# Cross attention on one core: the hand-written order of the first batch rewritten, one step of the last batch moved, nine warming products instead of ten

## The chip, the cores and the metric

The kernel runs on one core of one Trainium2 chip. The metric is the device time of one execution in microseconds (us). The engines of the core work side by side, each through its own list in order: TensorE (PE, matrix products into PSUM banks), VectorE (DVE), ScalarE (ACT), GpSimd (POOL, here reductions across partitions and accumulating transfers) and SyncE (SP, which issues most transfers). They wait for one another through semaphores.

## The reference

Eight batches of one cross-attention layer, all in float32. `x` and the context are (8, 512, 1024).

```python
q = jnp.einsum('bcn,dc->bnd', x1, Wq) + bq
k = jnp.einsum('bcn,dc->bdn', x2, Wk) + bk[:, None]
v = jnp.einsum('bcn,dc->bdn', x2, Wv) + bv[:, None]
attn = jax.nn.softmax(jnp.einsum('bnd,bdm->bnm', q, k), axis=2)
attn_out = jnp.einsum('bcm,bnm->bcn', v, attn)
return attn_out + x1
```

The width of q and k is 64, the softmax runs over the 1024 positions m, in eight blocks of 128.

## The kernel before, in words

A batch is a set of small steps, each a method of class `Batch` of one or a few instructions. Three strings, FIRST (batch 0), MIDDLE (batches 1 to 6) and LAST (batch 7), list the steps in program order; `follow` (called at the end of the kernel function) runs through the words. A word is a step and its indices; "+" ahead of it means the next batch, "-" the one before. The scheduling is manual: what the strings say is each engine's order. Two words on different engines have no order between them but that of their data and buffers.

The steps, by engine:

- TensorE. `VF.j.c` (line 373) is a float32 product for value block j in the first batch, one quarter c of the contraction, two recorded products each; blocks 0, 1 and 2 of batch 0 go this way. All other values take three passes of float32r with operands split in parts: `VY.j` (one pass, four products into a Y bank) and `VX.j` (two passes, eight products into an X bank). `K` and `Q` (line 204) project keys and queries with 64 output columns. `S.h.i` (line 261) makes scores of query half h and key block i. `RF.u.m` (line 458) is the float32 product of weights and values for query units 0 and 1 of batch 0; `R.u.m` (line 433) does three passes for the others.
- ScalarE. `wh`, `w4`, `xh`, `H`, `vh`, `qr`, `kr` round the high parts. `ke` and `qe` take K and Q out of PSUM. `Sc` copies scores to SBUF (line 266). `E` is the exponential (line 292), `es.Q` copies half of a query quarter Q for its sum, `sy` seeds a Y bank with the bias (line 389), `cy` and `oy` take Y banks out, `r2`, `of`, `os` scale.
- VectorE. `wl`, `wd`, `xl`, `xd`, `vl`, `vd`, `l`, `d`, `ql`, `kl` make the low and the combined parts. `jf` and `jn` join the banks to a value block. `F.Q` folds the scores of a quarter to a maximum (lines 274 to 277), `L.u` subtracts the maximum from unit u (line 289), `a2` and `a3` add up (line 318), `rec` inverts (line 337), `o` joins an output (line 498).
- POOL. `T.Q` reduces the maximum over the partitions (line 281), `tot.Q` the sum (line 328). `a1.Q` issues an accumulating transfer that adds the second half of the quarter's weights onto `es` (line 314), and `oa.u` one that adds x to an output (line 513). `a2.Q` on VectorE needs the landing of `a1.Q`, `T.Q` needs `F.Q`, and `L` needs `T`.
- SP. `ldx1`, `ldx2`, `lwq`, `lsd` load; `qd` and `kc` repeat q and k on the other 64 partitions; `few.Q` brings the sums into a column, and `rec.Q` needs it; `st.u` stores an output and waits for `oa.u`'s landing.

Buffers are counted in `BUFS`: X and Y banks three each, score banks two, the parts of weights and x five, five and four, outputs three. In batch 0 the odd `S` steps borrow Y banks. A bank or buffer goes to its next user in program order when its last reader is done; so o.7 on VectorE frees an X bank that VX.2 of batch 1 takes, and a small buffer that cy.1 takes.

In `begin`, x and weights are issued in quarters on the queues of ScalarE and SP, and ten products on zeros (4, 3 and 3, in three Y banks, line 533) keep TensorE at work until they land. `apart` says which half of chunk 1 of x is split in parts in batch 0, block 3 alone, since block 2 goes through `VF`.

The batches overlap: S, the maxima and some parts of batch b + 1 are made during the R steps of batch b.

Of the kernel before, what the change touches and what calls it, by code (L numbers as in the profile page):

```python
# [583 lines left out]
```

## Time and profile before

| | |
|---|---|
| median of three executions | 661.95 us (661.65 to 662.42) |
| the profiled execution, its own time | 662.4 us |
| its span, first to last instruction | 660.6 us |
| granted TensorE clock in the span | 1.00 |
| ScalarE busy | 450.8 us (68%) |
| GpSimd busy | 199.1 us (30%) |
| moved by DMA | 90.21 MB, 137 GB/s on average |

The span is shorter than the execution's own time, since it leaves out what lies before the first and after the last instruction. In the views, a row of the timeline begins with the start and the duration in us, then engine, line, operation, output<-input, shapes and count; in brackets stand the idle time just before it and what ended that. A row of the waits says who waited for whom, then us in total, times, and the longest. Rows of matrix products overlap by their modelled ends, so starts are compared and not durations.

### The profile page before, as it was taken

The page shows a single profiled execution, that of the slowest core. Times are in us where ns is not written, and L with a number is a line of the kernel's source. Part 1 is how long each engine was busy: PE and PEld are TensorE (multiplying, and loading weights), DVE is VectorE, ACT ScalarE, POOL GpSimd, SP SyncE. Part 2 cuts the span into 40 slices and gives each one's busy share as a digit, 9 for nine tenths or more (in the row PEclk, how much of TensorE's full clock was granted, in tenths as well). Part 3 has the DMA queues.
Part 4 walks back from the last instruction along what each step waited for, and adds up shares of the span by engine and source line. Part 5 has one row for each costly group of instructions (what it writes and reads, how often), then busy time and mean ns, then how long its engine had stood idle before and what let it go on. Part 6 is the DMA issues. An engine that isn't in the chain of part 4 may idle for free.

```text
span 660.6 us, 8048 instructions
## 1 busy us (share of the span) xinstructions
PE 653.9 (99%) x2798; PEld 491.8 (74%) x2798; DVE 617.3 (93%) x689; ACT 450.8 (68%) x668; POOL 199.1 (30%) x162
## 2 busy tenths in 40 slices
...
GB/s 301 208 139 86 79 121 213 82 197 92 126 175 106 180 99 145 141 162 128 116 151 116 216 101 112 172 84 223 81 127 175 82 206 96 127 114 48 62 144 130
DMA packets 41464, 90.21 MB, mean 137 GB/s; under 512 B 13136, under 2 KB 13904, under 8 KB 37712
## 3 DMA queue, kind: packets, MB, share of 16 engines
...
## 4 chain that ended last, share of the span: by engine, by line
PE 77%; DVE 13%; ACT 4%; DMA 3%; issue 2%; POOL 0%; SPq 0%; DVEq 0%; POOLq 0%; ACTq 0%
PE ps_oX L433 27%; PE ps_oY L433 14%; PE ps_vX L393 13%; PE ps_s L261 7%; PE ps_vY L393 7%; PE ps_k L204 3%; PE ps_q L204 3%; DVE e L289 3%; DVE el L300 2%; PE ps_v L373 2%; DVE vd L425 1%; DVE ed L305 1%; DVE vl L420 1%; DVE max L276 1%; DMA out_dram<-o 1%
## 5 line engine op out<-in xcount | busy, mean ns | idle before, releaser
L433 PE MATMUL ps_oY<-vd,ed 128*128 128x512 f32 x496 | 193.9, 393 | 0.2 <-DVE ed L305 0.2
L433 PE MATMUL ps_oX<-vh,eh 128*128 128x512 f32 x496 | 193.0, 389 | 0.0
L433 PE MATMUL ps_oX<-vl,el 128*128 128x512 f32 x496 | 193.0, 389 | 0.0
L433 PEld LDWEIGHTS ps_oY<-vd,ed 128*128 128x128 f32 x496 | 93.1, 188 | 25.1 <-issue 5.1
L513 POOL DMA_DIRECT2D o<-in_x1T_dram x62 | 56.0, 929 | 174.5 <-ACT o L510 100.4
L433 PEld LDWEIGHTS ps_oX<-vl,el 128*128 128x128 f32 x496 | 93.0, 188 | 20.3
L433 PEld LDWEIGHTS ps_oX<-vh,eh 128*128 128x128 f32 x496 | 93.1, 188 | 19.4 <-issue 0.2
L292 ACT ACTIVATE e<-e 128x1024 f32<-128x1024 f32 x64 | 68.0, 1062 | 49.8 <-DVE e L289 48.5
L266 ACT COPY e<-ps_s 128x512 f32<-128x512 f32 x128 | 70.7, 591 | 29.1 <-PE ps_s L261 28.2
L328 POOL PARTITION_ALL_REDUCE den<-es x32 | 79.3, 2477 | 21.2 <-DVE es L318 18.2
L314 POOL DMA_DIRECT2D es<-e x32 | 28.8, 901 | 188.3 <-ACT es L311 174.0
L305 DVE SCALAR_TENSOR_TENSOR ed<-el,eh 128x1024 fp32r<-128x1024 f32 x62 | 80.2, 1294 | 2.0
L300 DVE TENSOR_TENSOR el<-e,eh 128x1024 fp32r<-128x1024 f32 x62 | 79.7, 1302 | 0.0
L289 DVE TENSOR_TENSOR e<-e,top 128x1024 f32<-128x1024 f32 x64 | 75.9, 1217 | 0.0
L408 ACT COPY vy<-ps_vY 128x512 f32<-128x512 f32 x61 | 36.0, 591 | 45.3 <-PE ps_vY L393 41.7
L393 PE MATMUL ps_vX<-wh,xh 128*128 128x512 f32 x244 | 66.2, 393 | 0.0
L281 POOL PARTITION_ALL_REDUCE top<-max x32 | 45.4, 1417 | 66.7 <-DVE max L277 66.7
L393 PE MATMUL ps_vX<-wl,xl 128*128 128x512 f32 x244 | 65.3, 389 | 0.0
L393 PE MATMUL ps_vY<-wd,xd 128*128 128x512 f32 x244 | 64.3, 391 | 0.7 <-ACT ps_vY L389 0.7
L296 ACT ACTIVATE eh<-e 128x1024 fp32r<-128x1024 f32 x62 | 64.4, 1054 | 0.4
L393 PEld LDWEIGHTS ps_vX<-wh,xh 128*128 128x128 f32 x244 | 45.2, 188 | 14.3 <-DVE max L276 4.1
L393 PEld LDWEIGHTS ps_vY<-wd,xd 128*128 128x128 f32 x244 | 45.4, 188 | 12.5 <-ACT ps_vY L389 2.5
...
## 6 DMA issues: line engine op xcount, KB each, us to landing
...
es<-e POOLq DMA_DIRECT2D x32, 512.0 KB, 4.9
out_dram<-o SPq DMA_DIRECT2D x63, 256.0 KB, 2.4
o<-in_x1T_dram POOLq DMA_DIRECT2D x62, 256.0 KB, 4.3
x<-in_x_dram SPq DMA_DIRECT2D x5, 512.0 KB, 9.8
k<-k SPq DMA_DIRECT2D x16, 128.0 KB, 2.2
q<-q SPq DMA_DIRECT2D x16, 128.0 KB, 2.3
w_raw<-in_wvT_dram SPq DMA_DIRECT2D x4, 256.0 KB, 3.8
```

The costliest lines, as they stand in the source:

```text
L261: nc.tensor.matmul(ps, k[:, ts(i, P)], self.qa[:, ts(h, H)], start=(z == 0), stop=(z == 1))
L266: nc.scalar.copy(self.half[h][:, :, i, :], self.ps[h, i].rearrange("p (q n) -> p q n", q=2))
L281: nc.gpsimd.partition_all_reduce(self.top[Q], self.fold[Q][:, 0, :], P, ReduceOp.max)
L289: nc.vector.tensor_tensor(e, e, top, ALU.subtract)
L292: nc.scalar.activation(self.unit(u), self.unit(u), AF.Exp)
L296: nc.scalar.activation(self.e[u]["h"], self.unit(u), AF.Copy, scale=SPLIT)
L300: nc.vector.tensor_tensor(self.e[u]["l"], self.unit(u), f32(self.e[u]["h"]), ALU.subtract)
L305: nc.vector.scalar_tensor_tensor(e["d"], f32(e["l"]), -T, f32(e["h"]), ALU.mult, ALU.add)
L328: nc.gpsimd.partition_all_reduce(self.den[Q], self.es[Q][:, 0, :], P, ReduceOp.add)
L393: nc.tensor.matmul(ps, self.c[j // 2][z][:, c, ts(j % 2, P)], w[z][:, c, :], start=(start and c == 0), stop=(stop and c == CT - 1), skip_g ...
L433: nc.tensor.matmul(ps, self.e[u][z][:, m, :], self.v[m // 2][z][:, m % 2, :], start=start, stop=stop, skip_group_check=True,)
L513: nc.gpsimd.dma_start(self.o[u], x1T[self.b, ts(u, P), :], accum_op=ALU.add)
```

## The change

All three strings hold the same words as before, each once; nothing is computed in another way.

- `begin` issues 3 + 3 + 3 warming products instead of 4 + 3 + 3.
- FIRST is written anew. On TensorE the steps VF of blocks 0 and 1 alternate by quarter, K comes before VF.1.3, VY.3 stands between K and Q, VX.6 comes ahead of the first score step, all of S.1 with VY.6, VX.7 and VY.7 comes before the first RF step. On ScalarE the three `sy` come before `ke`, `vh.0` right behind it, `sy.7`, E.0, E.1 and es.0 behind six score copies. On VectorE `vl.0` and `vd.0` come right behind jf.1, `jn.5` ahead of F.0, vl.2 right behind it, a2.0 right behind l.3, d.2 and d.3 later; o.2 and o.3 stand together, o.5 stands ahead of the next batch's L steps. On SP ldx1.1 of the next batch goes ahead of ldx1.0, ldx2.0 behind qd, few.0 ahead of kc, st.1 and few.1 ahead of st.0. On POOL T.2 goes ahead of a1.1, T.3 ahead of a1.2, oa.1 first and oa.0 behind tot.1.
- In LAST, H.3 moves on ScalarE's list from behind es.2 to behind Sc.1.7, ahead of os.7 of the batch before. No other engine's order changes there.
- `apart` names its chunk through a constant, WHOLE = 3, with the same value 1 as before.

```diff
 FIRST = """
-VF.0.0 VF.0.1 VF.1.0 wh.0 wl.0 wd.0 w4.0 VF.1.1 wh.1 VF.0.2 wl.1 VF.0.3 w4.1 ldx2.0 xh.1 xl.1 xd.1 VF.1.2
-VF.1.3 wd.1 VF.2.0 VF.2.1 VF.2.2 VF.2.3 lwq ldx2.1 lsd K xh.2 xh.3 ldx1.0 bv ke xl.2 xl.3 ldx1.1 jf.0 jf.2
-xd.3 sy.3 sy.4 sy.5 jf.1 Q kc VY.3 qe kr cy.3 vh.0 qd kl VX.3 jn.3 vh.1 qr +ldx1.0 VX.5 VX.4 xd.2 VY.4 VY.5
-cy.4 cy.5 vl.1 ql S.0.0 S.0.1 S.0.2 S.0.3 Sc.0.0 Sc.0.1 vd.1 S.0.4 Sc.0.2 Sc.0.3 Sc.0.4 jn.4 S.0.5 Sc.0.5
-S.0.6 Sc.0.6 vl.0 vd.0 S.0.7 Sc.0.7 F.0 T.0 S.1.1 VX.6 sy.6 VY.6 cy.6 jn.6 jn.5 vh.2 S.1.0 Sc.1.0 Sc.1.1 L.0
-E.0 +ldx1.1 +Q +qe S.1.2 Sc.1.2 S.1.3 Sc.1.3 VX.7 S.1.4 Sc.1.4 RF.0.0 RF.0.1 S.1.6 F.1 S.1.7 S.1.5 RF.0.2
-RF.0.3 RF.0.4 L.1 E.1 es.0 RF.0.5 +ldx2.1 Sc.1.5 Sc.1.6 Sc.1.7 vl.2 vd.2 T.1 L.2 L.3 E.3 F.2 RF.1.0 H.3 l.3
-d.3 RF.1.1 RF.1.2 +ldx2.0 +K a1.0 a2.0 a3.0 E.2 H.2 es.1 l.2 a1.1 sy.7 VY.7 +qd +qr +ql RF.1.3 RF.1.4 RF.1.5
-d.2 cy.7 jn.7 RF.0.6 RF.1.6 RF.0.7 RF.1.7 +ke +kc R.2.0 vh.3 T.2 L.4 L.5 E.4 E.5 H.4 H.5 F.3 tot.0 few.0 rec.0
-r2.0 of.0 of.1 oa.0 oa.1 st.0 l.4 R.2.1 R.2.2 R.2.3 R.2.4 R.2.5 R.3.0 R.3.1 es.2 a1.2 a2.1 a3.1 R.3.2 R.3.3
-d.4 vl.3 R.3.4 +kr +kl +S.0.0 +S.0.1 +Sc.0.0 +Sc.0.1 R.3.5 +S.0.2 +Sc.0.2 +S.0.3 +Sc.0.3 vd.3 R.2.6 R.3.6
-R.2.7 R.3.7 +S.0.5 T.3 L.6 L.7 E.6 E.7 H.6 l.5 d.5 R.4.0 R.4.1 a2.2 tot.1 few.1 rec.1 r2.1 a3.2 tot.2 few.2
-es.3 a1.3 l.6 st.1 oy.2 o.2 oa.2 st.2 H.7 d.6 +S.0.4 +Sc.0.4 +Sc.0.5 l.7 oy.3 o.3 oa.3 st.3 R.4.2 R.4.3 R.4.4
-R.4.5 R.4.6 R.4.7 +S.0.7 d.7 +S.0.6 +Sc.0.6 +Sc.0.7 +F.0 +xh.0 +xl.0 +xd.0 a2.3 rec.2 r2.2 oy.4 +T.0 +L.0 +L.1
-o.4 oa.4 st.4 R.5.0 R.5.1 R.5.2 R.5.3 R.5.4 R.5.5 R.5.6 R.5.7 oy.5 o.5 oa.5 st.5 a3.3 +E.1 +F.1 +xh.2 +xl.2
-R.6.0 R.6.1 R.6.2 R.6.3 R.6.4 R.6.5 R.6.6 R.6.7 oy.6 o.6 R.7.0 R.7.1 R.7.2 R.7.3 +sy.0 +xh.1 +xl.1 +xd.1 +E.0
-+es.0 +sy.1 +S.1.0 +S.1.1 +xd.2 +xh.3 +Sc.1.0 +xl.3 +Sc.1.1 tot.3 few.3 rec.3 R.7.4 R.7.5 R.7.6 R.7.7 oy.7 o.7
+wh.0 VF.0.0 VF.1.0 wl.0 VF.0.1 VF.1.1 wd.0 w4.0 wh.1 VF.0.2 VF.1.2 wl.1 VF.0.3 wd.1 w4.1 ldx2.0 lwq VF.2.0
+xh.1 VF.2.1 xl.1 VF.2.2 xd.1 VF.2.3 ldx2.1 lsd xh.2 xh.3 bv xl.2 xl.3 jf.0 jf.2 xd.2 xd.3 sy.3 sy.4 sy.5 K ke
+VF.1.3 jf.1 vh.0 vl.0 vd.0 ldx1.0 VY.3 cy.3 ldx1.1 Q kc qe kr qd kl VY.4 cy.4 VX.4 jn.4 VX.3 jn.3 qr ql VY.5
+cy.5 VX.5 jn.5 vh.1 vl.1 VX.6 S.0.0 Sc.0.0 S.0.1 Sc.0.1 S.0.2 Sc.0.2 S.0.3 Sc.0.3 S.0.4 Sc.0.4 S.0.5 Sc.0.5
+vd.1 S.0.7 +ldx1.1 S.0.6 Sc.0.6 Sc.0.7 F.0 T.0 vh.2 vl.2 +ldx1.0 S.1.1 L.0 F.1 sy.6 L.1 S.1.0 Sc.1.0 Sc.1.1
+vd.2 +Q +qe +ldx2.1 S.1.2 Sc.1.2 VY.6 cy.6 jn.6 S.1.3 Sc.1.3 S.1.4 Sc.1.4 S.1.5 Sc.1.5 T.1 L.3 S.1.6 Sc.1.6
+VX.7 S.1.7 sy.7 VY.7 E.0 RF.0.0 RF.0.1 RF.0.2 RF.0.3 RF.0.4 RF.0.5 E.1 es.0 RF.1.0 a1.0 L.2 Sc.1.7 F.2 T.2
+RF.1.1 E.3 H.3 l.3 a2.0 RF.1.2 RF.1.3 E.2 H.2 es.1 l.2 a1.1 a3.0 +qd +qr +ql RF.1.4 cy.7 jn.7 vh.3 +ldx2.0 +K
++ke RF.1.5 L.5 E.5 RF.0.6 L.4 E.4 H.4 RF.1.6 d.2 RF.0.7 RF.1.7 R.2.0 vl.3 tot.0 few.0 rec.0 r2.0 of.1 oa.1 F.3
+of.0 d.3 es.2 R.2.1 R.2.2 R.2.3 R.2.4 R.2.5 R.3.0 R.3.1 R.3.2 R.3.3 R.3.4 a2.1 a3.1 +kc +kr +kl +S.0.0 +S.0.2
++Sc.0.0 H.5 l.4 R.3.5 st.1 +S.0.1 +Sc.0.1 +Sc.0.2 vd.3 R.2.6 R.3.6 T.3 L.6 L.7 E.7 +S.0.3 +Sc.0.3 R.2.7 R.3.7
+d.4 R.4.0 R.4.1 a1.2 a2.2 +S.0.4 +S.0.5 tot.1 few.1 rec.1 oa.0 st.0 a3.2 l.5 d.5 E.6 H.6 l.6 d.6 tot.2 few.2
+r2.1 oy.2 oy.3 o.2 o.3 oa.2 oa.3 st.2 st.3 H.7 l.7 rec.2 +Sc.0.4 +Sc.0.5 R.4.2 R.4.3 R.4.4 R.4.5 R.4.6 R.4.7
++S.0.6 +Sc.0.6 d.7 +S.0.7 +Sc.0.7 +F.0 es.3 a1.3 r2.2 oy.4 o.4 oa.4 st.4 +xh.0 +xl.0 +xd.0 +xh.1 +xl.1 R.5.0
+R.5.1 R.5.2 R.5.3 R.5.4 R.5.5 R.5.6 R.5.7 oy.5 o.5 +T.0 +L.0 +L.1 +E.0 +E.1 +es.0 oa.5 st.5 a2.3 a3.3 +F.1
++xd.1 R.6.0 R.6.1 R.6.2 R.6.3 R.6.4 R.6.5 R.6.6 R.6.7 oy.6 o.6 +S.1.0 +xh.2 +xl.2 +xd.2 +sy.0 R.7.0 R.7.1
+R.7.2 R.7.3 +xh.3 +xl.3 tot.3 few.3 rec.3 +sy.1 +Sc.1.0 +S.1.1 +Sc.1.1 R.7.4 R.7.5 R.7.6 R.7.7 oy.7 o.7
 """
...
 LAST = """
...
-l.1 S.1.6 Sc.1.5 Sc.1.6 a3.1 d.1 vh.2 vl.2 tot.0 few.0 sy.7 S.1.7 Sc.1.7 F.2 -os.7 -oa.7 -st.7 VX.7 VY.6 cy.6
+l.1 S.1.6 Sc.1.5 Sc.1.6 a3.1 d.1 vh.2 vl.2 tot.0 few.0 sy.7 S.1.7 Sc.1.7 F.2 H.3 -os.7 -oa.7 -st.7 VX.7 VY.6
...
-r2.0 vl.3 vd.3 R.0.6 R.1.6 R.0.7 R.1.7 T.2 L.4 L.5 E.4 E.5 es.2 H.3 d.2 R.2.0 R.2.1 R.2.2 R.2.3 R.2.4 R.2.5
+rec.0 r2.0 vl.3 vd.3 R.0.6 R.1.6 R.0.7 R.1.7 T.2 L.4 L.5 E.4 E.5 es.2 d.2 R.2.0 R.2.1 R.2.2 R.2.3 R.2.4 R.2.5
...
-        for i, times in enumerate((4, 3, 3)):
+        for i, times in enumerate((3, 3, 3)):
```

5 lines of the change are left out of this document (3 added, 2 removed).

## The prediction

> **What bounds the kernel now.** I read the page first, then TensorE's waits, then the rows of the batch starts, then VectorE between them.
>
> ```profile
> PE 653.9 (99%) x2798; PEld 491.8 (74%) x2798; DVE 617.3 (93%) x689; ACT 450.8 (68%) x668; POOL 199.1 (30%) x162
> ```
> ```profile
> PE ps_s L261 <- DVE kl L254: 0.7, 1, 0.7
> PE ps_vY L393 <- ACT ps_vY L389: 0.7, 2, 0.4
> PE ps_s L261 <- ACT e L266: 0.5, 2, 0.3
> ```
> TensorE is busy 99% of the span, and its visible waits after the start add to about 2 us. The change multiplies the same matrices, so it can only win or lose through such waits and what they stretch. Where are they? The first product of each batch after the first (VY.0, first row for batch 1, then 2 and 3) shows it:
>
> ```profile
> 102.67 1.07 PE L393 MATMUL ps_vY<-wd,xd 128*128 128x512 f32 x4
> ...
> 185.29 0.39 PE L393 MATMUL ps_vY<-wd,xd 128*128 128x512 f32 x1
> ...
> 265.54 0.61 PE L393 MATMUL ps_vY<-wd,xd 128*128 128x512 f32 x2
> ```
> Batch 1 lasts 82.62 us (185.29 - 102.67), batch 2 lasts 80.25. Both follow the same list of words, so batch 1 loses 2.37 us because the first batch hands it a late VectorE. That is the sum that a new first batch can win. VectorE from its first step after the first fold to the last output of batch 0:
>
> ```profile
> 38.71:109.16 70.45, 70.45 (x281) 48.63 (x278) 68.29 (x76) 50.03 (x72) 26.09 (x21) 1.00 0.56 129
> ```
> ```profile
> 38.71 1.29 DVE L411 SCALAR_TENSOR_TENSOR v<-ps_vX,vy 128x512 f32<-128x512 f32 x2 [1.01 <-ACT vy L408]
> ...
> 82.35 0.75 DVE L498 SCALAR_TENSOR_TENSOR o<-ps_oX,r,oy 128x512 f32<-128x512 f32 x1 [0.51 <-ACT oy L484]
> ...
> 108.36 0.17 DVE L337 RECIPROCAL r<-few 128x2 f32<-128x2 f32 x1 [0.52 <-DMA few<-den]
> ```
> The third busy figure, 68.29 of 70.45, is VectorE's. It runs without a break except for 0.51 and 0.52 us inside and 1.01 us ahead of the stretch. So batch 0 ends when VectorE has worked off its list, and o.7, which frees the banks and buffers that batch 1 wants, is done at about 109.16. The chain of work that ended last says what held the third of these waits:
>
> ```profile
> 96.98 5.39 DMA o<-in_x1T_dram
> ...
> 103.34 4.92 DMA few<-den
> ```
> The store st.5 waits on SP for oa.5's landing, few.3 stands behind st.5, and rec.3 and o.7 wait for few.3.
>
> **The change part by part.** *One warming product less.*
>
> ```profile
> 0.98 4.45 PE L533 MATMUL ps_warm<-warm 128*128 128x512 bf16 x10 [0.98 <-DVE spark L528]
> ```
> ```profile
> w_raw<-in_wvT_dram SPq DMA_DIRECT2D x1, 256.0 KB, 3.5
> x<-in_x_dram ACTq DMA_DIRECT2D x1, 128.0 KB, 3.7
> ```
> Ten products take 4.45 us, about 0.43 each. A later product of 512 columns takes 0.23 (1.81 us for eight, rows below), so TensorE runs at about half speed here, and work moved into this time counts half. VF.0.0 starts up to 0.43 us sooner but slowly: bounds 0 and 0.43, I take 0.21, half of it. Its first pieces of weight and x are issued at once at the start and land 3.5 and 3.7 us after, before nine products end. VF.1.0, now second, needs the same pieces, so the interleaved order asks the transfers for less. The other orders of VF change no number. The Trainium skill (TensorE: Matmul & The Clock Gate, section "Part 1: The HAM clock gate") says that the cold time is a window in time and not a count of products, and gives 426.7 ns for 512 cold columns. The row agrees (4.45 / 10); by that rule too the clock rises no sooner.
>
> *K, VF.1.3, VY.3 and Q apart; VX.6 ahead of S.0.0.*
>
> ```profile
> 22.75 1.20 PE L393 MATMUL ps_vY<-wd,xd 128*128 128x512 f32 x4
> ...
> 31.04 0.40 PE L261 MATMUL ps_s<-qa,kh 128*128 128x512 f32 x1
> ...
> 35.18 1.07 PE L393 MATMUL ps_vX<-wh,xh 128*128 128x512 f32 x4
> 36.08 1.07 PE L393 MATMUL ps_vX<-wl,xl 128*128 128x512 f32 x4
> 36.99 1.07 PE L393 MATMUL ps_vY<-wd,xd 128*128 128x512 f32 x4
> ```
> ```profile
> 31.78 4.03 ACT L266 COPY e<-ps_s 128x512 f32<-128x512 f32 x8
> ```
> ```profile
> 37.28 0.42 DVE L277 TENSOR_TENSOR max<-max 128x256 f32<-128x256 f32 x1
> ```
> Four products right behind Q are drawn 0.13 longer (1.20 against 1.07). K and Q, one block before, are now two, so I charge 0.2 for one more way in and out (bounds 0 and 0.4). VX.6 takes 1.81 (36.99 - 35.18). S.0.0 then starts at 31.04 + 1.81 + 0.2 - 0.21 = 32.84. Its copies began 0.74 after it and took 4.03, so they end at 37.6. The last third of F.0 must follow them (0.7 + 0.4), so F.0 ends at 38.7 to 38.8 instead of 37.7. The 1.8 us that S is later have paid for work ahead of it: vl.0 and vd.0 fill VectorE's early gaps, so ql is ready at about 30.4 (Q 0.9 later, its repeat by DMA as before), over 2 us ahead of S.0.0.
>
> *VectorE behind F.0.* It does the same list less jn.5, done before (half of the 1.29 row: 0.6). Before, it was occupied 70.45 - 0.51 - 0.52 = 69.42 us. The wait of 1.01 for cy.6 goes, as vl.2 stands behind F.0 and jn.6 far later. The wait of 0.51 at o.2 goes, because oy.2 and oy.3 now come right after H.6, while l.6 and d.6 run. The wait of 0.52 for few.3 goes: between +F.0 and o.5 there now stand o.4, two xl and one xd (0.7 and three of 1.15: 4.1 us) instead of xl, xd, two L, a2.3 and o.4 (four of 1.15, 0.6 and 0.7: 5.9), so oa.5, st.5 and few.3 come some 1.8 us sooner. What is late next is the list itself.
>
> *New overlaps with POOL.* Reductions on POOL stretch VectorE:
>
> ```profile
> 55.89 2.17 DVE L300 TENSOR_TENSOR el<-e,eh 128x1024 fp32r<-128x1024 f32 x1
> 58.09 2.00 DVE L237 TENSOR_TENSOR qa<-q,qa 64x1024 fp32r<-64x1024 f32 x1
> ```
> ```profile
> 56.10 1.34 POOL L281 PARTITION_ALL_REDUCE top<-max  x1
> 57.34 2.38 POOL L328 PARTITION_ALL_REDUCE den<-es  x1
> ```
> ```profile
> 80.61 1.22 DVE L300 TENSOR_TENSOR el<-e,eh 128x1024 fp32r<-128x1024 f32 x1
> ```
> ```profile
> 80.85 2.63 POOL L328 PARTITION_ALL_REDUCE den<-es  x1 [6.27 <-DVE es L318]
> ```
> Under T.2 and tot.0 the two steps took 4.17 where two of the kind take 2.3: 1.87 for 3.72 us of reduction, half. Under tot.2 it cost nothing, as l.6 was running first and VectorE then waited. In the new order T.0 has vl.2 beside it (+0.4; before, VectorE idled) and tot.2 has l.5 and d.5 (+0.9); T.2 now falls on F.2's end, l.3 and a2.0 and should cost less (-0.6). Sum +0.7; bounds -1.9 (tot.0 goes free as tot.2 did) and +2.0 (all eight reductions cost half).
>
> *New wait: a2.0 for a1.0.* a2.0 moves from behind d.3 to right behind l.3, and l.2, a3.0, ql, jn.7 and d.2 queue behind it.
>
> ```profile
> es<-e POOLq DMA_DIRECT2D x1, 512.0 KB, 4.8
> ```
> ```profile
> es<-e POOLq DMA_DIRECT2D x1, 512.0 KB, 7.1
> ```
> The first row is a1.0 of before, the second a1.2. ScalarE gets to the end of es.0 at about 49.1: +Q ends at 41.1, qe at 42.5, then six half-us copies with sy.7 and E.0, E.1, es.0 at 1 us each. a1.0 lands at 49.2 + 4.8 = 54.0; VectorE, 13.9 us of steps and 0.7 to 1 of stretch behind 38.8, wants it at 53.4 to 53.7 (two folds of 2.6, seven steps of 1.15, jn.6). I charge 0.3; bounds 0 and 2.8 (at 7.1).
>
> *Queues.* On SP, ldx1.1 goes ahead of ldx1.0, ldx2.0 behind qd, few.0 ahead of kc, st.1 and few.1 ahead of st.0; on POOL, T.2 passes a1.1, T.3 passes a1.2, and oa.0 drops behind tot.1. Covers: Q is wanted 3 us after both halves, K over 4, tot.0 ends before ke. If a cover failed the price is a wait of VectorE, as for a2.0. On TensorE the closest new dependences are RF.0.0 on E.0 (0.4 us of room), +S.0.3 on the bank of +Sc.0.2 (near none) and R.5.0 on o.2 (0.8); a fraction of a us lost there is absorbed as long as VectorE ends batch 0.
>
> *Last batch: H.3 earlier on ScalarE.*
>
> ```profile
> 624.74 2.00 ACT L296 ACTIVATE eh<-e 128x1024 fp32r<-128x1024 f32 x2
> ```
> ```profile
> 626.18 1.22 DVE L300 TENSOR_TENSOR el<-e,eh 128x1024 fp32r<-128x1024 f32 x1
> ```
> H.3 is the first of the two; its reader l.3 starts in its turn, with no wait. Moving it saves nothing, and its 1 us ahead of os.7 stands mostly before cy.6's wait for TensorE. I take 0; bounds -0.1 and +0.4.
>
> **The sum.** VectorE ends batch 0 at 38.8 + 69.42 - 0.6 + 0.7 + 0.3 = 108.6 instead of 109.16. That lead of about 0.55 us comes off the 2.37 us of batch 1, and the rest stays. The profiled execution (span 660.6, 662.4 with what lies around) would take 661.85; it stands 0.45 above the median of 661.95, so the median becomes **661.4**.
>
> **The rivals.** *All of it goes (faster).* If the reductions fall as tot.2 did and a1.0 is in time, the lead is 0.55 + 0.3 + 1.5 or more, and the 2.37 us go: 659.6. For it speaks that later batches show no such loss; against it, that VectorE is 97% busy in the stretch above (68.29 of 70.45). *few.3 again (no change).* If o.5 is not sooner, oa.5's 5.39 and few.3's 4.92 still end at 108.3 and o.7 goes as before: 661.9. Against it speak the 1.8 us worked out above. *a2.0 waits (slower).* If a1.0 takes the 7.1 us of the second row, VectorE stands 2.8 us instead of 0.3, batch 0 ends 1.95 later: 663.9. It decides from a landing of 5.35 us (no gain) and costs over 0.2% from 6.7. For it: transfers of POOL's queue took 4.8 to 7.1 in this batch, and two loads of x are under way. *Whole blocking (slower).* If each reduction stopped VectorE for all its time, T.0 and tot.2 would add 1.34 + 2.38, as in the rows of POOL above, instead of 0.4 + 0.9: 2.4 us worse, 663.8. Those rows, half in one place and nothing in another, speak against it. The Trainium skill (SBUF — State Buffer, section "Who interferes with whom") has this rule: a VectorE instruction with two SBUF inputs and a GpSimd one that reads SBUF exclude each other, whichever starts first.
>
> **How the numbers follow.** Forecast 0.45, all of it gone 0.24, few.3 again 0.12, a2.0 waits 0.14, whole blocking 0.05. The range reaches from the full 2.37 (659.6) to just short of the a2.0 case: 663.7. A measurement of this kernel tells about 0.2%, 1.3 us, from no change. Faster by that needs a lead of 1.3: the second case and a bit of the first, 0.30. Slower: the last two and a bit of the first, 0.21. Within: 0.49.
>
> **What would show it.** Right: VY.0 of batch 1 at 102 to 103, o.7 ending near 108.6, batch 1 lasting 81.5 to 82.2, S.0.0 at 32.8, F.0 ending at 38.8, l.5 or d.5 stretched under tot.2, no wait at rec.3, the last batch as before. Wrong: a wait of VectorE for es of over 1 us, idle time of TensorE inside batch 0, or batch 1 as long as before.

## The result, and the profile after

The changed kernel takes 661.24 us (median of 14 runs, 659.66 to 662.31), the kernel before 662.54 beside it (14 runs, 661.65 to 663.16). The ratio is 0.9976, with a 95% interval of 0.9968 to 0.9985: faster by 0.24%, which lies just beyond the 0.2% that a measurement of this kernel can tell from no change, with an interval that reaches to both sides of that bound. The forecast was 661.4 and "within 0.2%" as the likeliest case. The time lies 0.2 us from the forecast; that two errors nearly met in it is shown at the end.

The profiled execution of after has a span of 657.9 us and takes 659.74, 2.7 us under the profiled one of before. It is one of the fastest of its kernel, so its gain is larger than that of the medians, 1.3; where the difference sits is shown below. First the lines of the page that answer to those shown of before: the busy time of the engines, and the chain that ended last, by engine, in after and then in before.

```profile
PE 652.4 (99%) x2797; PEld 491.6 (75%) x2797; DVE 615.3 (94%) x689; ACT 451.0 (69%) x668; POOL 204.6 (31%) x162
...
PE 94%; DVE 3%; ACT 2%; issue 0%; DVEq 0%; ACTq 0%
```
```profile
PE 77%; DVE 13%; ACT 4%; DMA 3%; issue 2%; POOL 0%; SPq 0%; DVEq 0%; POOLq 0%; ACTq 0%
```
TensorE is as busy as before (99%). The chain now runs for 94% of the span through TensorE's own products, where it was 77% before; VectorE's share fell from 13% to 3%, and the transfers' 3% are gone. Then TensorE's waits in after:

```profile
PE ps_warm L535 <- DVE spark L530: 1.0, 1, 1.0
PE ps_vY L395 <- ACT ps_vY L391: 0.4, 1, 0.4
PE ps_s L263 <- ACT e L268: 0.2, 1, 0.2
PE ps_oY L435 <- DVE ed L307: 0.2, 1, 0.2
```
The wait of 0.7 for kl is gone, and one of the two for a seeded bank. What is left stands in the last batch. The starts of VY.0 in batches 1, 2 and 3 of after (start, duration, engine and line, operation):

```profile
102.08 1.07 PE L395 MATMUL ps_vY<-wd,xd 128*128 128x512 f32 x4
...
182.66 1.07 PE L395 MATMUL ps_vY<-wd,xd 128*128 128x512 f32 x4
...
262.91 1.07 PE L395 MATMUL ps_vY<-wd,xd 128*128 128x512 f32 x4
```
Batch 0 ends 0.59 us sooner (102.67 before), batch 1 lasts 80.58 instead of 82.62, and batch 2 lasts 80.25 as before. The 2.37 us that batch 1 lost have shrunk to 0.33, and from batch 2 on after stands 2.63 us ahead and keeps it to the end (span 660.6 and 657.9). So the new last batch brought nothing, and all of the gain was made before 182.66. VectorE of after, in the stretch from its first step behind the first fold to the end of o.7 (third busy figure), and the steps in it that answer to the forecast:

```profile
38.59:107.49 68.90, 68.90 (x276) 48.24 (x273) 66.20 (x76) 49.68 (x73) 29.61 (x21) 1.00 0.59 136
```
```profile
38.59 1.22 DVE L422 SCALAR_TENSOR_TENSOR vl<-vh,v 128x1024 fp32r<-128x1024 f32 x1
40.77 1.22 DVE L291 TENSOR_TENSOR e<-e,top 128x1024 f32<-128x1024 f32 x1 [0.96 <-POOL top L283]
...
54.47 0.69 DVE L320 TENSOR_TENSOR es<-es 128x512 f32<-128x512 f32 x1 [0.61 <-DMA es<-e]
...
56.66 1.22 DVE L239 TENSOR_TENSOR qa<-q,qa 64x1024 fp32r<-64x1024 f32 x1
57.91 0.69 DVE L413 SCALAR_TENSOR_TENSOR v<-ps_vX,vy 128x512 f32<-128x512 f32 x1
58.52 2.53 DVE L291 TENSOR_TENSOR e<-e,top 128x1024 f32<-128x1024 f32 x2
...
78.91 2.00 DVE L307 SCALAR_TENSOR_TENSOR ed<-el,eh 128x1024 fp32r<-128x1024 f32 x1
...
107.49 0.68 DVE L413 SCALAR_TENSOR_TENSOR v<-ps_vX,vy 128x512 f32<-128x512 f32 x1
```
```profile
38.77 1.96 POOL L283 PARTITION_ALL_REDUCE top<-max  x1 [38.34 <-DVE max L279]
...
52.90 1.88 POOL L283 PARTITION_ALL_REDUCE top<-max  x1 [2.50 <-DVE max L279]
...
56.73 2.81 POOL L330 PARTITION_ALL_REDUCE den<-es  x1 [0.99 <-DVE es L320]
...
77.90 2.62 POOL L330 PARTITION_ALL_REDUCE den<-es  x1 [5.36 <-DVE es L320]
```
The step that follows o.7 starts at 107.49; before, at 109.16. The lead is 1.67 us, three times the forecast 0.55. The waits for cy.6, oy.2 and few.3 are gone, as forecast. A wait of 0.96 for T.0 is new and was not forecast. The wait for a1.0 is 0.61. Under tot.0 (56.73 to 59.54), where before two steps of 1.2 took 2.0 and more, ql is clean at 1.22 and jn.7 comes next; of two L steps in 2.53 about 0.2 is stretch (two clean ones take 2.35). Under tot.2 d.5 takes 2.00, as forecast.

### The profile page after: what moved, and what is told of

It reads as the page before. It is cut to its first block, busy times and chain, and to the rows that moved or that the text cites. A ratio compares the mean times of both kernels' runs of the same rounds, so it can differ in the third digit from the quotient of the medians.

```text
span 657.9 us, 8049 instructions
## 1 busy us (share of the span) xinstructions
PE 652.4 (99%) x2797; PEld 491.6 (75%) x2797; DVE 615.3 (94%) x689; ACT 451.0 (69%) x668; POOL 204.6 (31%) x162
## 4 chain that ended last, share of the span: by engine, by line
PE 94%; DVE 3%; ACT 2%; issue 0%; DVEq 0%; ACTq 0%
PE ps_oX L435 33%; PE ps_oY L435 17%; PE ps_vX L395 15%; PE ps_s L263 8%; PE ps_vY L395 8%; PE ps_k L206 4%; PE ps_q L206 4%; PE ps_o L460 2%; PE ps_v L375 2%; PE ps_warm L535 1%; DVE vd L427 1%; DVE vl L422 0%; DVE v L413 0%; ACT ps_vY L391 0%; DVE ed L307 0%; DVE e L291 0%
## 5 line engine op out<-in xcount | busy, mean ns | idle before, releaser
L294 ACT ACTIVATE e<-e 128x1024 f32<-128x1024 f32 x64 | 67.7, 1061 | 54.7 <-DVE e L291 53.6
L330 POOL PARTITION_ALL_REDUCE den<-es x32 | 82.1, 2565 | 23.3 <-DVE es L320 20.2
L307 DVE SCALAR_TENSOR_TENSOR ed<-el,eh 128x1024 fp32r<-128x1024 f32 x62 | 81.9, 1321 | 2.1
L291 DVE TENSOR_TENSOR e<-e,top 128x1024 f32<-128x1024 f32 x64 | 76.1, 1220 | 1.0 <-POOL top L283 1.0
L283 POOL PARTITION_ALL_REDUCE top<-max x32 | 46.8, 1463 | 65.3 <-DVE max L279 65.2
```

The costliest lines, as they stand in the source:

```text
L291: nc.vector.tensor_tensor(e, e, top, ALU.subtract)
L294: nc.scalar.activation(self.unit(u), self.unit(u), AF.Exp)
L307: nc.vector.scalar_tensor_tensor(e["d"], f32(e["l"]), -T, f32(e["h"]), ALU.mult, ALU.add)
L330: nc.gpsimd.partition_all_reduce(self.den[Q], self.es[Q][:, 0, :], P, ReduceOp.add)
```

## The experiments

**Theory A** (the prediction's): VectorE's list up to o.7 decides when batch 1 can go on, and TensorE's time follows it. **A1**, within it: the list got shorter because POOL's reductions T.2 and tot.0 now fall beside other steps of VectorE. **Rival B**: the products that TensorE is given, and their order, decide, and VectorE's waits are echoes of that. Two smaller questions were what the warming product and the last batch are worth. Each timed run stood beside runs of the kernel before on the same chip; these had medians of 662.34, 662.58 and 662.17 us in the three sets (e1 to e4, e5 to e8, e9 to e12).

One table serves all of them. From the trace of each profiled execution it has three times: the start of K (with the old first batch less 0.9, since there the two products of VF.1.3, 0.45 each, stand ahead of K and now behind it); the start of VectorE's step behind o.7; and VY.0 of batch 2.

| kernel | first batch | ratio to before (95%) | K | behind o.7 | less K | VY.0 of batch 2 | less o.7 |
|---|---|---|---|---|---|---|---|
| before | old | 1 | 14.83 | 109.16 | 94.33 | 185.29 | 76.13 |
| e1_warm9 | old | 0.9995 (0.9986 to 1.0004) | 15.27 | 109.54 | 94.27 | 185.65 | 76.11 |
| e3_last | old | 0.9999 (0.9991 to 1.0008) | 15.47 | 109.72 | 94.25 | 185.83 | 76.11 |
| e7_pe_twice | old | 1.0011 (1.0002 to 1.0019) | 14.28 | 108.76 | 94.48 | 185.37 | 76.61 |
| e11_red_alone | old | 1.0067 (1.0055 to 1.0080) | 14.18 | 112.93 | 98.75 | 189.04 | 76.11 |
| after | new | 0.9976 (0.9968 to 0.9985) | 14.23 | 107.49 | 93.26 | 182.66 | 75.17 |
| e2_first | new | 0.9975 (0.9966 to 0.9984) | 15.39 | 108.64 | 93.25 | 183.82 | 75.18 |
| e4_again | new | 0.9972 (0.9961 to 0.9983) | 14.79 | 108.72 | 93.93 | 183.85 | 75.13 |
| e5_undo_red | new | 0.9990 (0.9982 to 0.9999) | 15.33 | 110.81 | 95.48 | 185.93 | 75.12 |
| e6_dve_twice | new | 1.0009 (1.0000 to 1.0018) | 14.04 | 109.85 | 95.81 | 185.18 | 75.33 |
| e8_filled | new | 0.9981 (0.9971 to 0.9991) | 14.73 | 108.53 | 93.80 | 183.63 | 75.10 |
| e9_sy0 | new | 0.9977 (0.9969 to 0.9986) | 13.86 | 107.41 | 93.55 | 182.56 | 75.15 |
| e10_sy0_warm8 | new | 0.9978 (0.9970 to 0.9987) | 13.86 | 108.88 | 95.02 | 184.04 | 75.16 |
| e12_dve_twice_sy0 | new | 1.0005 (0.9996 to 1.0014) | 14.39 | 110.28 | 95.89 | 185.57 | 75.29 |

The last column is the finding to read first. Whatever was done to the kernel here, batch 2 starts 75.1 to 75.3 us behind o.7 with the new first batch, and 76.1 with the old one (76.6 where TensorE was given more to do). o.7 moved over a range of 5.5 us, and everything behind it came along. That is theory A, with a constant of about 0.96 us on top that goes with the order. The start of TensorE is not absorbed, though: in before, e1_warm9 and e3_last the step behind o.7 starts 94.25 to 94.33 behind K, whenever K starts.

**The parts alone: e1_warm9, e2_first, e3_last, e4_again.** The first is the kernel before with this one line changed:

```
-        for i, times in enumerate((4, 3, 3)):
+        for i, times in enumerate((3, 3, 3)):
```


> The order of before with nine warming products, nothing else. Theory A (VectorE's list in batch 0 sets the end, TensorE's start is absorbed): VectorE's steps ahead of F.0 do not wait for TensorE in the order of before, so the time moves by 0 to -0.2 us, and batch 1 still lasts about 82.6 us. Theory B (the earlier start of TensorE is the gain): -0.5 us or more, all of it visible at the first product of batch 1.

The second is the kernel before with the text of FIRST from after (ten products, the old last batch):

```
 FIRST = """
-VF.0.0 VF.0.1 VF.1.0 wh.0 wl.0 wd.0 w4.0 VF.1.1 wh.1 VF.0.2 wl.1 VF.0.3 w4.1 ldx2.0 xh.1 xl.1 xd.1 VF.1.2
+wh.0 VF.0.0 VF.1.0 wl.0 VF.0.1 VF.1.1 wd.0 w4.0 wh.1 VF.0.2 VF.1.2 wl.1 VF.0.3 wd.1 w4.1 ldx2.0 lwq VF.2.0
...
```


> Only the new FIRST; ten warming products and the old LAST. Theory A: nearly the whole gain of the change, -1.0 to -1.4 us in the median, with batch 1 at 80.5 to 82 us. Theory B: no more than half of it, -0.6 us or less, since the earlier start is missing.

The third is the kernel before with the text of LAST from after:

```
-l.1 S.1.6 Sc.1.5 Sc.1.6 a3.1 d.1 vh.2 vl.2 tot.0 few.0 sy.7 S.1.7 Sc.1.7 F.2 -os.7 -oa.7 -st.7 VX.7 VY.6 cy.6
+l.1 S.1.6 Sc.1.5 Sc.1.6 a3.1 d.1 vh.2 vl.2 tot.0 few.0 sy.7 S.1.7 Sc.1.7 F.2 H.3 -os.7 -oa.7 -st.7 VX.7 VY.6
...
```


> Only the new LAST: H.3 earlier on ScalarE. Theory A: 0 within 0.2 us, because its reader l.3 on VectorE starts in its turn in both traces. Rival (ScalarE's list in the last batch gates the end): -0.5 us or more.

The fourth is after, once more.

> The changed kernel once more, beside the parts on the same chip. Expected -1.3 us against before, like the result. If the parts add up, e1 + e2 + e3 gives the same sum. A profile of an execution that lies about 1.5 us above the best ones should show either a longer stretch of VectorE under a reduction of POOL in batch 0, or kl of batch 1's successor (L256) again behind tot.1; under theory B it should show a later start of the full TensorE clock instead.

The medians: e1_warm9 662.06 us, e2_first 660.41, e3_last 662.47, e4_again 660.67. The new first batch alone has the whole gain (somewhat more than the 1.0 to 1.4 us expected of it), the last batch has none, and the three parts add up to after within the intervals. The warming product is too small for the medians (ratio 0.9995, 0.9986 to 1.0004); the trace shows it where two executions agree in all else. e1_warm9 and e3_last differ in it alone up to K, and both reach full product speed at the same time (6.76 and 6.74 us by the trace's records of the clock); the row of K in e1_warm9, then in e3_last:

```profile
16.17 3.65 PE L204 MATMUL ps_k<-x,wqk_sb 128*64 128x512 f32 x16
```
```profile
16.37 3.65 PE L204 MATMUL ps_k<-x,wqk_sb 128*64 128x512 f32 x16
```
The difference is 0.20, the 0.21 of the prediction. But before's own K starts at 15.73 and after's at 14.23: K's start moves by more than the product is worth, from execution to execution. What moves is the time at which TensorE comes to full speed. Products of VF between 4.9 and 6.4 us, grouped (count, busy, mean ns of one), in e1_warm9 and then in after:

```profile
L373 PE MATMUL ps_v<-w_raw,x 128*128 128x512 f32 x2 | 1.9, 1061 | 0.0
```
```profile
L375 PE MATMUL ps_v<-w_raw,x 128*128 128x512 f32 x4 | 1.9, 592 | 0.0
```
Both have nine warming products. In that stretch the one takes 1061 ns for a product, the other 592. Of after's lead over before 0.6 us stand at K already (14.83 and 14.23): 0.2 are the product, 0.4 this accident. e4_again, the same kernel as after, was expected to show a longer stretch under a reduction, or a late +kl, if its execution was a slower one. It shows neither: half of its 1.2 us are a later full speed (which the expectation had left to rival B), the other half is a wait of VectorE at o.5, shown further down.

**The reductions: e5_undo_red, e11_red_alone.** The first is after with T.2 and a3.0 moved so that T.2 and tot.0 run back to back beside l.2, ql and their neighbours, as before:

```
-VX.7 S.1.7 sy.7 VY.7 E.0 RF.0.0 RF.0.1 RF.0.2 RF.0.3 RF.0.4 RF.0.5 E.1 es.0 RF.1.0 a1.0 L.2 Sc.1.7 F.2 T.2
-RF.1.1 E.3 H.3 l.3 a2.0 RF.1.2 RF.1.3 E.2 H.2 es.1 l.2 a1.1 a3.0 +qd +qr +ql RF.1.4 cy.7 jn.7 vh.3 +ldx2.0 +K
+VX.7 S.1.7 sy.7 VY.7 E.0 RF.0.0 RF.0.1 RF.0.2 RF.0.3 RF.0.4 RF.0.5 E.1 es.0 RF.1.0 a1.0 L.2 Sc.1.7 F.2
+RF.1.1 E.3 H.3 l.3 a2.0 RF.1.2 RF.1.3 E.2 H.2 es.1 a3.0 l.2 a1.1 T.2 +qd +qr +ql RF.1.4 cy.7 jn.7 vh.3 +ldx2.0 +K
```


> The changed kernel with two steps put back: T.2 behind a1.1 on GpSimd, a3.0 ahead of l.2 on VectorE, so that T.2 and tot.0 run one behind the other under l.2 and ql as before the change. Theory A1 (the lead of VectorE came from where the reductions fall): VectorE's steps from l.2 to L.4 are stretched by 1.0 to 1.7 us more, o.7 ends that much later, and of it the part that batch 1 cannot absorb shows: +0.9 to +1.6 us against the changed kernel, about -0.3 to -0.9 against before. Rival A2 (the lead came from jn.5 and the waits that went): within 0.3 us of the changed kernel.

It took 662.12 us, ratio 0.9990 (0.9982 to 0.9999): about 0.9 us of the gain is gone (0.0014 of 662). That is the lower end of what was expected, and the two intervals just overlap, 0.9982 and 0.9985; four other measurements of the new first batch lie at 0.9972 to 0.9978. In its trace ql is stretched again, by the reductions beside it; VectorE's steps, then POOL's:

```profile
57.59 1.21 DVE L302 TENSOR_TENSOR el<-e,eh 128x1024 fp32r<-128x1024 f32 x1
58.84 2.00 DVE L239 TENSOR_TENSOR qa<-q,qa 64x1024 fp32r<-64x1024 f32 x1
```
```profile
56.51 1.34 POOL L283 PARTITION_ALL_REDUCE top<-max  x1
57.77 2.70 POOL L330 PARTITION_ALL_REDUCE den<-es  x1
```
Counted from K, the end of o.7 is 2.22 us later than in after (95.48 and 93.26). But 0.90 of it is a wait of VectorE at another place, o.5:

```profile
97.60 0.75 DVE L500 SCALAR_TENSOR_TENSOR o<-ps_oX,r,oy 128x512 f32<-128x512 f32 x1 [0.90 <-PE ps_oX L435]
```
The row names TensorE, but the last product for o.5 had started at 91.69. It is most likely the wait for an output buffer that e10_sy0_warm8 shows below. What is left is 1.3 by the trace, against 0.9 by the medians: A1 holds, with about this size. The second does the same move the other way round, in the kernel before:

```
-RF.0.3 RF.0.4 L.1 E.1 es.0 RF.0.5 +ldx2.1 Sc.1.5 Sc.1.6 Sc.1.7 vl.2 vd.2 T.1 L.2 L.3 E.3 F.2 RF.1.0 H.3 l.3
-d.3 RF.1.1 RF.1.2 +ldx2.0 +K a1.0 a2.0 a3.0 E.2 H.2 es.1 l.2 a1.1 sy.7 VY.7 +qd +qr +ql RF.1.3 RF.1.4 RF.1.5
-d.2 cy.7 jn.7 RF.0.6 RF.1.6 RF.0.7 RF.1.7 +ke +kc R.2.0 vh.3 T.2 L.4 L.5 E.4 E.5 H.4 H.5 F.3 tot.0 few.0 rec.0
+RF.0.3 RF.0.4 L.1 E.1 es.0 RF.0.5 +ldx2.1 Sc.1.5 Sc.1.6 Sc.1.7 vl.2 vd.2 T.1 L.2 L.3 E.3 F.2 T.2 RF.1.0 H.3 l.3
+d.3 RF.1.1 RF.1.2 +ldx2.0 +K a1.0 a2.0 E.2 H.2 es.1 l.2 a3.0 a1.1 sy.7 VY.7 +qd +qr +ql RF.1.3 RF.1.4 RF.1.5
+d.2 cy.7 jn.7 RF.0.6 RF.1.6 RF.0.7 RF.1.7 +ke +kc R.2.0 vh.3 L.4 L.5 E.4 E.5 H.4 H.5 F.3 tot.0 few.0 rec.0
```


> The kernel before with two words moved: T.2 right behind F.2, and a3.0 from ahead of l.2 to behind it. If the placing of POOL's reductions against VectorE's two-input steps is what the new first batch won (theory A1), VectorE ends batch 0 by 0.3 to 1.0 us sooner and the time falls by 0.2 to 1.0. If it needs the rest of the new order with it (rival: T.2 and tot.0 then fall on other two-input steps, or on the wait for a1.0), o.7 ends within 0.2 us of the 109.16 of before, allowing for the start of K, and the time stays within 0.3.

It missed both expectations: 666.33 us, ratio 1.0067 (1.0055 to 1.0080). The two words alone cost 4.2 us. POOL's row of T.2 in e11_red_alone and the a1.0 and a1.1 behind it, and VectorE's a2.0:

```profile
52.72 1.89 POOL L281 PARTITION_ALL_REDUCE top<-max  x1 [6.99 <-DVE max L277]
54.48 1.97 POOL L314 DMA_DIRECT2D es<-e  x2
```
```profile
59.95 0.69 DVE L318 TENSOR_TENSOR es<-es 128x512 f32<-128x512 f32 x1 [4.72 <-DMA es<-e]
```
In before, a1.0 was issued on POOL at 48.60. Here it stands behind T.2 in POOL's queue, and T.2 waits for F.2's last step until 52.7, so a1.0 is issued at 54.5 and VectorE waits 4.72 for it. In the new first batch a1.0 stands ahead of F.2 and T.2. The two words are worth what they are only in their place in the whole order.

**Which engine: e6_dve_twice, e7_pe_twice.** In the first, after's VectorE does d.6 and d.7 twice, 2.3 us more, with the same values:

```
-            nc.vector.scalar_tensor_tensor(e["d"], f32(e["l"]), -T, f32(e["h"]), ALU.mult, ALU.add)
+            for _ in range(2 if self.first and u in (6, 7) else 1):
+                nc.vector.scalar_tensor_tensor(e["d"], f32(e["l"]), -T, f32(e["h"]), ALU.mult, ALU.add)
```


> The changed kernel with d.6 and d.7 of batch 0 done twice each: 2.3 us more on VectorE, the same output. Theory A: o.7 of batch 0 ends 2.3 us later while VY.0 of batch 1 stays at its place, and batch 1 grows: +1.9 to +2.3 us against the changed kernel. Rival B (TensorE's list sets the end, VectorE has room): at most +0.3.

In the second, before's TensorE does four pairs of products of S of batch 1 twice (they run within batch 0), 1.82 us more, with the same values:

```
-            for z, k in enumerate((self.kh, self.klow)):
+            twice = self.b == 1 and h == 0 and i >= 4
+            for z, k in 2 * list(enumerate((self.kh, self.klow))) if twice else enumerate((self.kh, self.klow)):
```


> The kernel before with the products of the scores +S.0.4 to +S.0.7 done twice, eight products more or 1.82 us on TensorE late in batch 0, the same output. Theory A: VY.0 of batch 1 comes 1.8 us later, but batch 1's first loss of about 1.3 us goes, since VectorE is then less late against TensorE: +0.3 to +0.8 us against before. Rival B: +1.8 us.

2.3 us of VectorE brought 663.01, ratio 1.0009 (1.0000 to 1.0018), against 0.9976 of after: 2.2 us. By the table VY.0 of batch 2, counted from K, comes 2.71 later (171.14 and 168.43). 1.82 us of TensorE brought 663.12, 0.5 over before (ratio 1.0011, 1.0002 to 1.0019), and by the table 0.63 (171.09 and 170.46). VectorE's work counts in full, and TensorE's by a third. The two additions stand in different kernels, after and before, so they are no strict pair; but if VectorE had room, as B says, the first could not cost 2.2 us. B falls. One part of the first expectation missed: VY.0 of batch 1 did not stay at its place but started at 103.86 (102.08 in after).

**The two new waits filled: e8_filled.** In after, vd.2 goes ahead of L.0 (which waits 0.96 for T.0), and d.3 ahead of a2.0 (which waits 0.61):

```
-vd.1 S.0.7 +ldx1.1 S.0.6 Sc.0.6 Sc.0.7 F.0 T.0 vh.2 vl.2 +ldx1.0 S.1.1 L.0 F.1 sy.6 L.1 S.1.0 Sc.1.0 Sc.1.1
-vd.2 +Q +qe +ldx2.1 S.1.2 Sc.1.2 VY.6 cy.6 jn.6 S.1.3 Sc.1.3 S.1.4 Sc.1.4 S.1.5 Sc.1.5 T.1 L.3 S.1.6 Sc.1.6
+vd.1 S.0.7 +ldx1.1 S.0.6 Sc.0.6 Sc.0.7 F.0 T.0 vh.2 vl.2 vd.2 +ldx1.0 S.1.1 L.0 F.1 sy.6 L.1 S.1.0 Sc.1.0 Sc.1.1
++Q +qe +ldx2.1 S.1.2 Sc.1.2 VY.6 cy.6 jn.6 S.1.3 Sc.1.3 S.1.4 Sc.1.4 S.1.5 Sc.1.5 T.1 L.3 S.1.6 Sc.1.6
...
-RF.1.1 E.3 H.3 l.3 a2.0 RF.1.2 RF.1.3 E.2 H.2 es.1 l.2 a1.1 a3.0 +qd +qr +ql RF.1.4 cy.7 jn.7 vh.3 +ldx2.0 +K
+RF.1.1 E.3 H.3 l.3 d.3 a2.0 RF.1.2 RF.1.3 E.2 H.2 es.1 l.2 a1.1 a3.0 +qd +qr +ql RF.1.4 cy.7 jn.7 vh.3 +ldx2.0 +K
...
-of.0 d.3 es.2 R.2.1 R.2.2 R.2.3 R.2.4 R.2.5 R.3.0 R.3.1 R.3.2 R.3.3 R.3.4 a2.1 a3.1 +kc +kr +kl +S.0.0 +S.0.2
+of.0 es.2 R.2.1 R.2.2 R.2.3 R.2.4 R.2.5 R.3.0 R.3.1 R.3.2 R.3.3 R.3.4 a2.1 a3.1 +kc +kr +kl +S.0.0 +S.0.2
```


> The changed kernel with its two waits of VectorE filled: vd.2 ahead of L.0 (which waits 0.96 us for T.0) and d.3 ahead of a2.0 (which waits 0.61 us for a1.0). o.7 should end 0.8 to 1.4 us earlier. Theory A with a cap: batch 1 of the changed kernel has only 0.33 us left to lose, so -0.2 to -0.4 us against the changed kernel. Rival (every us of VectorE counts): -0.8 us or more.

It missed: 660.96 us, ratio 0.9981 (0.9971 to 0.9991), and o.7 ends 0.54 later from K than in after. The two waits are gone, and others have come in their place; VectorE's L.2 and L.3, and later +kl, of e8_filled:

```profile
47.58 2.36 DVE L291 TENSOR_TENSOR e<-e,top 128x1024 f32<-128x1024 f32 x2 [0.35 <-POOL top L283]
...
69.13 2.70 DVE L256 TENSOR_TENSOR kl<-k,kh 128x1024 fp32r<-128x1024 f32 x1 [0.42 <-ACT kh L252]
```
+kl now waits for ScalarE and then takes 2.70 instead of 1.22, beside a reduction. A shorter wait at one place moved VectorE against POOL's reductions at the next.

**VY.0's seed: e6_dve_twice's wait, e9_sy0, e12_dve_twice_sy0, e10_sy0_warm8.** In e6_dve_twice TensorE's wait stood at VY.0 of batch 1, for ScalarE's seed of its bank:

```profile
103.86 1.20 PE L396 MATMUL ps_vY<-wd,xd 128*128 128x512 f32 x4 [1.34 <-ACT ps_vY L392]
```
In the new order +sy.0 stands on ScalarE behind +E.0, +E.1 and +es.0, which wait for VectorE's +L.0 and +L.1. If that is the place at which VectorE's lateness reaches TensorE, an earlier seed should win something. e9_sy0 is after with +sy.0 earlier; e12_dve_twice_sy0 is e6_dve_twice with the same edit, where the stake is larger:

```
-R.5.1 R.5.2 R.5.3 R.5.4 R.5.5 R.5.6 R.5.7 oy.5 o.5 +T.0 +L.0 +L.1 +E.0 +E.1 +es.0 oa.5 st.5 a2.3 a3.3 +F.1
-+xd.1 R.6.0 R.6.1 R.6.2 R.6.3 R.6.4 R.6.5 R.6.6 R.6.7 oy.6 o.6 +S.1.0 +xh.2 +xl.2 +xd.2 +sy.0 R.7.0 R.7.1
+R.5.1 R.5.2 R.5.3 R.5.4 R.5.5 R.5.6 R.5.7 oy.5 +sy.0 o.5 +T.0 +L.0 +L.1 +E.0 +E.1 +es.0 oa.5 st.5 a2.3 a3.3 +F.1
++xd.1 R.6.0 R.6.1 R.6.2 R.6.3 R.6.4 R.6.5 R.6.6 R.6.7 oy.6 o.6 +S.1.0 +xh.2 +xl.2 +xd.2 R.7.0 R.7.1
```


> The changed kernel with the seed of VY.0's bank (+sy.0 on ScalarE) moved from behind +xh.2 to right behind oy.5, ahead of +E.0, +E.1 and +es.0, which wait for VectorE's +L.0 and +L.1. Theory V (VectorE's lateness reaches TensorE through this seed): the wait of 0.4 us of VY.0 for the seed goes, and the time is 0.2 to 0.6 us under that of the changed kernel (ratio to before 0.9967 to 0.9973). Rival W (the wait at VY.0 only stands in for another one, of VX.0 for o.7's banks, right behind it): the wait moves to another row of the same place and the time stays within 0.2 us of the changed kernel's.

> The kernel of e6_dve_twice (2.3 us more work for VectorE in d.6 and d.7) with +sy.0 right behind oy.5 as in e9_sy0. Theory V: the wait of 1.34 us of VY.0 for the seed goes, and the time falls by 0.8 to 1.5 us against e6_dve_twice's 663.0. Rival W: as the banks that o.7 frees are late by the same amount, a wait of about 1 us shows at VX.0 or at a later product of batch 1, and the time falls by less than 0.5.

e9_sy0 took 660.64 us, ratio 0.9977 (0.9969 to 0.9986), the same as after. It had little to win: after's profile has no wait at VY.0 of batch 1, and the 0.4 that the expectation names stands in the last batch, at 598.11. So e12_dve_twice_sy0 is the test. It took 662.38, ratio 1.0005 (0.9996 to 1.0014), not to be told from e6_dve_twice (1.0009, 1.0000 to 1.0018). Its TensorE waits:

```profile
PE ps_vY L396 <- ACT ps_vY L392: 0.7, 2, 0.4
PE ps_vX L396 <- DVE o L501: 0.7, 1, 0.7
```
The wait of 1.34 is gone and VY.0 starts 1.2 us sooner (102.68), but VX products of batch 1 now wait 0.7 for an output of VectorE, and batch 2 starts no sooner behind o.7 (75.29 and 75.33). Theory V of the expectations falls and W holds: the seed was a place where the wait showed, not its cause. e10_sy0_warm8 has eight warming products besides:

```
-        for i, times in enumerate((3, 3, 3)):
+        for i, times in enumerate((3, 3, 2)):
```


> The kernel of e9_sy0 with eight warming products (3, 3, 2). If the first pieces of weight and x are still there in time, VF.0.0 comes 0.43 us sooner at half speed and the time falls by 0.2 us more, inside the interval; the first product should start at 4.3 and TensorE should not wait for a DMA. If the pieces land after 4.3, the wait shows ahead of VF.0.0 and nothing is won.

660.55 us, ratio 0.9978 (0.9970 to 0.9987): nothing that can be told from after. No wait for the first pieces of weight or x shows, but K starts at 13.86 as in e9_sy0, so the product less won nothing there either. The profiled execution shows another wait, at o.5:

```profile
95.67 0.75 DVE L500 SCALAR_TENSOR_TENSOR o<-ps_oX,r,oy 128x512 f32<-128x512 f32 x1 [1.66 <-DMA out_dram<-o]
```
o.5 writes into a buffer that is free only when an earlier store has left it. This wait is 1.66 here, 0.57 in e4_again, 0.22 in e9_sy0 and, if the reading above is right, 0.90 in e5_undo_red; there is none in the profiled executions of after and e2_first, and none in the five with the old order. There o.5 stood behind the next batch's two L steps. The new order has it ahead of them, which was to take away the wait for few.3, and brings this one into some executions. Without it, o.7 lies 93.25 to 93.36 behind K in all five executions whose VectorE list is that of after. That after's profiled execution has none of it is one reason why it is among the fastest of its kernel: e4_again, the same kernel, has 0.56 from a later K and 0.57 from this wait, and its VY.0 of batch 2 is 1.19 later (183.85 and 182.66).

## Why the prediction came out right, point by point

The forecast of the time was right; the sum behind it was right in kind and wrong in its sizes. Its lead of VectorE had five terms, which by the rows of before and after measure as follows: forecast first, measured second, in us.

| term | forecast | measured |
|---|---|---|
| end of F.0 (37.7 before) | +1.1 | +0.89 (38.59) |
| waits for cy.6, oy.2, few.3 | -2.04 | -2.04 (none is left) |
| jn.5 done before | -0.6 | -0.6 (not measured by itself) |
| new waits | +0.3 | +1.57 (0.96 for T.0, 0.61 for a1.0) |
| POOL's reductions | +0.7 | -1.49 (what is left: 69.42 - 0.6 less 68.90 - 1.57) |
| sum | -0.55 | -1.67 |

- **The failed step is "New overlaps with POOL".** It gave the reductions +0.7 within bounds of -1.9 to +2.0, and the rows give -1.49. It priced T.0, T.2 and tot.2 and left the others where they had been. Added up from VectorE's rows (the time from one step's start to the next, less that of a clean step), the stretch under each reduction is, in us:

| reduction | charged | before | after | change |
|---|---|---|---|---|
| T.2 | -0.6 | 1.06 | 0.09 | -0.97 |
| tot.0 | 0 | 0.90 | 0.31 | -0.59 |
| T.3 | 0 | 0.53 | 0.98 | +0.45 |
| tot.2 | +0.9 | 0.08 | 0.90 | +0.82 |
| tot.3 | 0 | 1.39 | 0.77 | -0.62 |
| the next batch's T.1 | 0 | 0.62 | 0.11 | -0.51 |
| T.0 and all the rest | +0.4 | 2.67 | 2.60 | -0.07 |

So tot.2 cost what was forecast (d.5 at 2.00 where 1.2 is clean). The error has two main parts. T.2 and tot.0 brought -1.56 where -0.6 was charged: T.2 (52.90 to 54.78) runs beside l.3, which stays clean, and while VectorE waits for a1.0; tot.0 begins just after ql and then stands beside jn.7, which reads a PSUM bank. And tot.3 with the next batch's T.1 brought -1.13 where nothing was charged. Half of that is one fold of F.1 under tot.3; VectorE of before, POOL of before, VectorE of after:

```profile
97.65 2.09 DVE L276 TENSOR_TENSOR max<-max,e 128x512 f32<-128x512 f32 x1
```
```profile
97.56 2.34 POOL L328 PARTITION_ALL_REDUCE den<-es  x1
```
```profile
99.00 1.47 DVE L278 TENSOR_TENSOR max<-max,e 128x512 f32<-128x512 f32 x1
```
The step is 0.69 when clean. e5_undo_red shows that the places of T.2 and tot.0 were worth 0.9 (medians) to 1.3 us (trace); the part at the end of the batch was not tried by itself. The bound of -1.9 ("tot.0 goes free") pointed the right way, but tot.0 did not go quite free, and much of the gain came elsewhere.
- **"New wait: a2.0 for a1.0"** was in the right place: 0.61 where 0.3 was charged. The landing that decides it was 5.1 us behind its issue at 49.35 (54.47), under the 5.35 at which the prediction saw the gain end. e11_red_alone shows the rival's mechanism in full: 4.72 of wait, 4.2 us of time.
- **Not seen: L.0's wait for T.0.** The prediction gave T.0 vl.2 for company and asked only what that stretches. It did not ask what VectorE does behind vl.2: L.0 needs T.0, T.0 takes 1.96, one step of 1.22 covers it badly, and 0.96 is idle. e8_filled shows that filling this gap and the next wins nothing here.
- **Not seen either: o.5's wait for its buffer.** The prediction counted on the earlier o.5 to end the wait for few.3 and did not ask whether an output buffer would be free that early. In after's profiled execution it is; in others the wait is up to 1.66.
- **K and Q apart.** S.0.0 starts at 32.59 (forecast 32.84): TensorE's earlier full speed brought it 0.4 forward, and the split cost 0.14 more than charged. From K to S.0.0 there are 18.36 us, 15.31 before; 1.81 are VX.6 and 0.9 VF.1.3, so the split costs 0.34 where 0.2 was charged, within its bounds of 0 and 0.4. The rows of K and of S.0.0 in after:

```profile
14.23 3.65 PE L206 MATMUL ps_k<-x,wqk_sb 128*64 128x512 f32 x16
```
```profile
32.59 0.39 PE L263 MATMUL ps_s<-qa,kh 128*128 128x512 f32 x1
```
- **The warming product** gave 0.20 where 0.21 was taken. **H.3** and the new last batch gave nothing, as taken (e3_last: 0.9999, 0.9991 to 1.0008).
- **"That lead comes off the 2.37 us of batch 1, and the rest stays"** held for the lead and failed for the rest. Beside the 1.67 of o.7 another 0.96 went in batch 1, by a meeting that the prediction did not look at: +kl, VectorE's step for the keys of batch 2, and batch 1's reduction tot.2 come at the same moment. VectorE of before, then POOL of before:

```profile
157.43 0.42 DVE L318 TENSOR_TENSOR es<-es 128x256 f32<-128x256 f32 x1
157.96 2.36 DVE L254 TENSOR_TENSOR kl<-k,kh 128x1024 fp32r<-128x1024 f32 x1
```
```profile
157.96 1.99 POOL L328 PARTITION_ALL_REDUCE den<-es  x1
```
The same in after:

```profile
155.78 0.42 DVE L320 TENSOR_TENSOR es<-es 128x256 f32<-128x256 f32 x1
156.11 1.22 DVE L256 TENSOR_TENSOR kl<-k,kh 128x1024 fp32r<-128x1024 f32 x1
157.25 2.12 DVE L307 SCALAR_TENSOR_TENSOR ed<-el,eh 128x1024 fp32r<-128x1024 f32 x1
```
```profile
156.30 2.68 POOL L330 PARTITION_ALL_REDUCE den<-es  x1
```
In before both are recorded from 157.96; +kl takes 2.36, twice its length, and TensorE's 0.7 us of wait for kl (first row of its waits in the prediction) is the price. TensorE around this wait, in before:

```profile
159.31 0.39 PE L261 MATMUL ps_s<-qa,kh 128*128 128x512 f32 x1
160.37 0.50 PE L261 MATMUL ps_s<-qa,kl 128*128 128x512 f32 x1 [0.68 <-DVE kl L254]
160.71 0.40 PE L261 MATMUL ps_s<-qa,kh 128*128 128x512 f32 x1
```
The starts lie 1.06 and 0.34 apart where 0.23 is the pace, together 0.94 too much; in after the same products keep the pace. In after +kl starts 0.19 ahead of the reduction and is clean, and d.5 behind it, for which TensorE does not wait, takes the stretch. In all five traces with the old first batch both start together and +kl is stretched; in all nine with the new one +kl is first. So it goes with the order and not with chance, and by its size it is the constant 0.96 of the table's last column, though no run changed this meeting alone. The Trainium skill (SBUF — State Buffer, section "Who interferes with whom") says that issue order decides which of the two blocks. This pair agrees (+kl takes 1.22 when it begins first, 2.36 when not); other rows do not, if the recorded starts are taken for the issue: l.2 of before begins at 55.89, 0.21 ahead of T.2, and takes 2.17, and kl of e8_filled above begins 0.22 ahead of its reduction (69.35) and takes 2.70.

**The rivals.** "All of it goes" is nearest to what the profiled execution shows: most of its mechanism came (tot.0 from 0.90 to 0.31), 2.04 of the 2.37 us went, and a1.0 was nearly in time. The medians show 1.3, and the later sets 1.5 to 1.9 for the new first batch (ratios of 0.9978 to 0.9972). The two come near each other once the accidents of the one execution are taken out: of 2.63 between the profiled ones, 0.4 are the earlier full speed of TensorE, and after's had no wait for a store at o.5 where e4_again had 0.57. That leaves 2.2, or 1.7 with that wait; the interval of the ratio is 1.0 to 2.1 us. "few.3 again" fell: nothing waits at rec.3. "a2.0 waits" did not come, but e11_red_alone shows that it can. "Whole blocking" fell in its size: under tot.2 of 2.62 us d.5 was stretched by 0.8, and the longest stretch in these rows is 1.5 (kl of e8_filled, beside a reduction of 2.10).

So the gain was underrated, 0.55 where the medians show 1.3, by a lead that was too small and a term of 0.96 that was missing. The forecast of the time still came within 0.2 us because it hung on a median of three runs of before, 661.95, and over 14 runs the same kernel has 662.54: the one error nearly made up for the other, which is luck. Judged by the ratio (0.9976 of 661.95 is 660.4) the forecast is 1.0 too high, within its range.
